# A two-layer graph network on one core: the last pair's reset gates by seven block products, the first load of x in two parts, and new scheduling constants

## The chip, the cores and the metric

The kernel runs on one core of a Trainium2 chip. The metric is device time in microseconds (us) for one execution; lower is better. A core has five instruction streams that matter here. TensorE (PE, with its weight loads as PEld) multiplies. VectorE (DVE), ScalarE (ACT) and GpSimd (POOL) work on elements. SyncE (SP) issues most of the DMAs; ScalarE's queue issues a few at the start. Each stream runs its instructions in the order in which they were written for it, and waits at the head when an input is not there yet.

## The reference, cut to what matters

The inputs are x (64 graphs, 256 nodes, 256 features) and a 0/1 adjacency of 64 matrices of 256 by 256. All arithmetic is float32.

```python
# layer 0
h = relu(bn(conv1d(xT, conv1_w)))                 # 1x1 convolution over the features
h = bn(conv1d(h, conv2_w, pad=8))                 # 17 taps over the nodes
x_conv = relu(h + xT).T
s = x @ w_se.T + b_se                             # 3 coordinates of each node
A = exp(-dist(s, s)) * adj
x_nmp = A @ relu(x @ w_msg.T + b_msg)             # message pass
x_in = concat([x_conv, x_nmp])
gi, gh = x_in @ w_ih.T + b_ih, x @ w_hh.T + b_hh  # each has parts r, z, n
r = sigmoid(gi_r + gh_r); z = sigmoid(gi_z + gh_z)
n = tanh(gi_n + r * gh_n)
x = layernorm(x + (1 - z) * n + z * x)
# layer 1
h = layernorm(x)
conv = (adj @ h) @ W_rel + b_rel + h @ W_root
out = layernorm(x + x + relu(conv))
```

## The kernel before, in words

**Tiling.** Activations lie transposed, features on the 128 partitions (two chunks, C = 2), nodes along the free axis. The 64 graphs are 8 blocks of 8; a block is 4 pairs, so there are 32 pairs. Pair 31 is the last one.

**Stages.** At the start `conv1(0)` reads the first block's x pair by pair (`fetch`, L811 to L827), transposes it on TensorE (`turned`, L829 to L848: eight transposes of 128x128 into two banks named `ps_xTc`, one ScalarE copy for each bank, one store to the buffer `xt` in memory), and runs the 1x1 convolution (`ps_c`, L866) with the weights `w1`. The weights and the batch norm's numbers (`chan`) come through ScalarE's DMA queue (L494, L495). Then `filters` turns the 17 taps into 47 filter matrices: weights `wt` are loaded, copied by VectorE (`ws`, L560), transposed (`ps_tT`, L569, copy on ScalarE L571), multiplied by a constant matrix (`ps_w`, L590) and evicted by ScalarE (L596); the result `w2m` is stored to memory. From then on, for each block, the 17-tap convolution is a transform of the activations (VectorE, L707 and others), 47 products with the filters (`ps_k`, L735) and a transform back. The filters are streamed in two-slot ring `cs` by SP's queue (`cs<-w2m`, 105 loads of 768 KB). Beside it, conv1 of the block after next runs.

**A pair.** `pair(p)` computes messages (`ps_msg`, L1105), distances (`ps_dist`, L1142), the exponential (ScalarE, L1146), the product with adj (VectorE, L1149), and the message pass (`ps_nmp`, L1156, evicted by ScalarE at L1158). Then come the gates. RG holds the reset gate and the hidden part of n; ZN holds the update gate and the input part of n. In the usual pairs the 2x2 block products of weights and activations are done as seven products instead of eight (`product`, L1198; banks `ps_a`, `ps_b`, `ps_d`): VectorE prepares differences of activation blocks (L1175 to L1183), ScalarE puts a bank into RG or ZN (`put`, L1220 and L1222), VectorE adds banks on (`onto`, L1226), and ScalarE applies the tanh by which the sigmoid is computed (`squash`, L1230). Pairs 0, 1 and 31 (PLAIN) use eight plain products (`products_of`, bank `ps_g`, L1194). For pair 31 (`apart`) these go graph by graph: RG and then ZN of graph 0, then RG and ZN of graph 1; ZN goes straight from its bank into the new state (`turn_in`, L1231 to L1241). Layer 1 follows: norm (x at L1364), projection (`ps_hy`, L1383; sums on VectorE L1385), aggregation (`ps_agg`, L1397; for the last nodes L1436) and the final norm and store (L1426, L1445, L1446). In pair 31 it goes graph by graph too.

**What sets the order.** All operations are recorded with a key, a due time in planned microseconds (`prog.at`). Pair p is due at FIRST_GATES + p * PERIOD; conv1, the convolution, filter loads and coordinates have keys relative to this through the constants at L58 to L68 (for instance COORDS, W_LAG, LOAD_AHEAD, CONV1_FROM). A list scheduler (`scheduled`) then writes a static order for each engine and each queue from these keys, its own cost model and the shares of the PSUM banks. So a changed constant can move any instruction.

Of the kernel before, what the change touches and what calls it, by code (L numbers as in the profile page):

```python
# [18 lines left out]
P = 128  # L19
B, N, D = 64, 256, 256  # L20
C = D // P
# [10 lines left out]
BG = 8  # L32
# [22 lines left out]
OB, OG = 3, 64  # L55
HQ = 2 * M * C * (M + 1)
XC_SLOTS = BG + 2
FIRST_GATES, PERIOD, GATE_TIME = 115.6, 58.9, 14.5  # L58
AHEAD_FROM, AHEAD_TO, W_DEEP = -43.5, -52.5, 2
CONV1_FROM, CONV1_TO, CONV_FROM, CONV_OUT, CONV_TO = -29.4, 98.8, -11.5, -38.6, -37.2  # L60
PAIR_LEAD, FILTER_LEAD, LOAD_AHEAD = 40.6, -2.5, 17.5
SMALL_RUNS, TURN_FROM = 1.3, 2
FILTERS_TO, STORES_AT = 51.5, 52.7
KEEP = 13.3
LATE_LAG = 28.4
W_FROM, W_LAG = 2, 41.9
COORDS = 40.5
PLAIN, SUMS_FROM = (0, 1, B // 2 - 1), 2  # L68


# [349 lines left out]
def gnn_two_layers(  # L420
# [32 lines left out]
    def bank(name, share="rest"):  # L453
        return Space(name, [P, 512], "psum", share, share if share in ("conv", "gate") else None).view
# [36 lines left out]
    taps = sb("taps", [P, NM * OB], "filters")  # L491

    prog.at(0.0)
    A.dma_start(out=chan_sb, in_=chan)  # L494
    A.dma_start(out=w1, in_=w1T.rearrange("(c p) n -> p c n", p=P))  # L495
    tb = np.zeros((2, OG, NM * OB), np.float32)
    tb[:, :TAPS * OB] = np.einsum("kf,op->kofp", tap_matrix(), np.eye(OB, dtype=np.float32)).reshape(TAPS * OB, NM * OB)
    tb = tb.reshape(P, NM * OB)
# [305 lines left out]
    def conv1(b):  # L804
        def edges(h):
            G.memset(h[:, :8, :, :, M:], 0.0)
            G.memset(h[:, 8:, :, :, :1], 0.0)
        XN = {}

        def fetch(g):  # L810
            if b >= TURN_FROM:  # L811
                XN[g] = xn_ahead[:, :4 * D]
                blocks = XN[g].rearrange("p (c k i) -> p c k i", c=C, i=SQ)
                rows_of = x[b * BG + g:b * BG + g + 2].rearrange("g (b j) d -> j (g b) d", j=SQ)
                with prog.group():
                    for a in range(P // SQ):
                        for c in range(C):
                            at = c * P + a * SQ
                            SP.dma_start(out=blocks[a * SQ:(a + 1) * SQ, c], in_=rows_of[:, :, at:at + SQ])
                return  # L820
            if b > 0:
                XN[g] = xn_ahead[:, :4 * D].rearrange("p (j d) -> p j d", d=D)
            elif g >= 4:
                XN[g] = W2[:, 1, 8 + 2 * g:12 + 2 * g]
            else:
                XN[g] = cs[:, g * 512:g * 512 + 1024].rearrange("p (j d) -> p j d", d=D)
            SP.dma_start(out=XN[g], in_=x[b * BG + g:b * BG + g + 2].rearrange("g (c p) d -> p (g c) d", p=P))  # L827

        def turned(g):  # L829
            xn = XN[g]  # L830
            if b >= TURN_FROM:
                V.transpose(xTc_ahead.rearrange("p c n -> p (c n)"), xn)
                SP.dma_start(out=xt_dram[(b * BG + g) // 2], in_=xTc_ahead)
                return xTc_ahead
            if b > 0 or g == 4:
                xTc = xTc_ahead
            elif g:
                xTc = W2[:, 1, 6 * g - 12:6 * g - 8].rearrange("p (c f) o -> p c (f o)", c=C)
            else:
                xTc = cs[:, 2048:3072].rearrange("p (c n) -> p c n", c=C)  # L840
            for c in range(C):
                ps = bank("ps_xTc")
                with prog.group():
                    for j in range(4):
                        PE.transpose(ps[:, j * P:(j + 1) * P], xn[:, j, c * P:(c + 1) * P], ident, hold=[xTc[:, c]])
                A.copy(xTc[:, c, :], ps)
            SP.dma_start(out=xt_dram[(b * BG + g) // 2], in_=xTc)
            return xTc  # L848

        if b == 0:  # L850
            for g in range(0, BG, 2):
                fetch(g)
                edges(HP[:, g // 2])
        for g in range(0, BG, 2):
            h = HP[:, g // 2]
            if b > 0:
                fetch(g)
            xTc = turned(g)
            if b > 0:
                h = xn_ahead.rearrange("p (j c g k) -> p j c g k", j=M, c=C, g=2)  # L860
                edges(h)
            for o in range(C):
                ps = bank("ps_c1")
                with prog.group():
                    for c in range(C):
                        PE.matmul(ps, w1[:, c, o * P:(o + 1) * P], xTc[:, c, :], start=(c == 0), stop=(c == C - 1),  # L866
                                  hold=[h[:, :, o]])
                pv = ps.rearrange("p (g t j) -> p j g t", g=2, j=M)
                for j, at in ((0, 0), (8, 1)):
                    A.activation(h[:, j:j + 8, o, :, at:at + M], pv[:, j:j + 8],  # L870
                                 AF.Relu, bias=bn_shift[0][:, o:o + 1], scale=bn_scale[0][:, o:o + 1])
            if b == 0:
                fold(g // 2)
            else:
                SP.dma_start(out=hd(b * BG // 2 + g // 2), in_=xn_ahead)
# [210 lines left out]
    def pair(p):  # L1086
# [75 lines left out]
        V.tensor_add(xc, xc, xT)  # L1162
        A.activation(xc, xc, AF.Relu)
        ins = (xT, nmp, xc)
        right = []
        for v, t, when in zip(ins, (tx, nmps, tc_), (due - 28, due - 10, due - 20)):
            prog.at(when, 0.3)
            b11, b12, b21, b22 = (v[:, c, g, :] for c in range(C) for g in range(2))
            if p in PLAIN:
                right.append((b11, b12, b21, b22))  # L1170
                continue
            t1, t2, t4 = (t[:, i, :] for i in ((0, 5, 6) if v is nmp else range(3)))
            t3 = t[:, 3, :] if v is xT else b12
            if v is xT:
                V.tensor_sub(t[:, 0::3], v[:, :, 1, :], v[:, 0])  # L1175
            elif v is nmp:
                V.tensor_sub(t[:, 0:3:2], t[:, 2:5:2], t[:, 1:3])
            else:
                V.tensor_sub(t1, b12, b11)
            V.tensor_sub(t2, b22, t1)  # L1180
            V.tensor_sub(t4, b21, t2)
            if v is xc:
                V.tensor_sub(t3, b22, b12)  # L1183
            right.append((b11, b21, b22, t4, t1, t2, t3))

        def products_of(ps, f, g, second, ks):
            gates = (((0, (0, 2, 1)), (2, (0,))), ((1, (0, 2, 1)), (2, (2, 1))))[second]
            with prog.group():
                for h, (gate, sources) in enumerate(gates):
                    for s in (s for s in sources if s in ks):  # L1190
                        for k in range(C):
                            left = (0, 1, 6, 3)[2 * f + k]
                            block = A21[0] if left == 6 else WB[:, left]
                            PE.matmul(ps[:, h * N:(h + 1) * N], block[:, s, gate, :], right[s][2 * k + g],  # L1194
                                      start=0 in ks and h == 0 and s == sources[0] and k == 0,
                                      stop=s == sources[-1] and k == C - 1, skip_group_check=True)

        def product(ps, i, second, start):  # L1198
            gates = (((0, (0, 2, 1)), (2, (0,))), ((1, (0, 2, 1)), (2, (2, 1))))[second]
            left, at = i, i  # L1200
            if p in PLAIN:
                f, k, g = i
                left, at = (0, 1, 6, 3)[2 * f + k], 2 * k + g
            block = A21[0] if p in PLAIN and left == 6 else WB[:, left]
            with prog.group():
                for h, (gate, sources) in enumerate(gates):
                    for j, s in enumerate(sources):
# [32 lines left out]
            stt(r, z, 3.0, r, op0=ALU.add, op1=ALU.mult)  # L1240
            stt(wT[:, i], n, 4.0, r)  # L1241

        if plain:
            prog.at(due, 2 * GATE_TIME / 44)
            for gs in ((0,), (1,)) if apart else ((0, 1),):
                for T in (RG, ZN):
                    for f in range(C):
                        for g in gs:
                            a = bank("ps_g", "gate")
                            for ks in ((0, 1), (2,)) if not apart else ((0, 1, 2),):  # L1250
                                products_of(a, f, g, T is ZN, ks)
                            if T is ZN and apart:
                                turn_in(f, g, a)
                            else:
                                put(T, f, g, a)
                        if not (T is ZN and apart):
                            squash(T, f, gs)
        else:
            for T in (RG, ZN):
                second = T is ZN  # L1260
                prog.at(due + second * GATE_TIME, GATE_TIME / 21)
                a = bank("ps_a", "gate")
                product(a, 0, second, True)
                put(T, 0, 0, a)
                b_ = bank("ps_b", "gate")
                product(b_, 1, second, True)
                onto(T, 0, 0, b_)
                product(a, 5, second, False)
                put(T, 0, 1, a)
                d = bank("ps_d", "gate")  # L1270
                product(d, 4, second, True)
                product(a, 6, second, False)
                put(T, 1, 1, a)
                onto(T, 1, 1, d)
                product(d, 2, second, False)
                onto(T, 0, 1, d)
                product(a, 3, second, False)
                put(T, 1, 0, a)
                for f in range(C):
                    squash(T, f, (0, 1))  # L1280

        prog.at(due + 2 * GATE_TIME, 0.3)
        pieces = [slice(0, 4)]
# [290 lines left out]
```

## Time and profile before

| | |
|---|---|
| median of 3 runs | 1990.72 us (1989.74 to 1990.74) |
| the profiled execution's own time | 1990.39 us |
| its span | 1988.6 us |
| granted TensorE clock, mean | 0.999 |
| TensorE busy | 1974.2 us (99%) |
| VectorE busy | 1710.0 us (86%) |
| ScalarE busy | 1006.7 us (51%) |
| GpSimd busy | 275.3 us (14%) |
| DMA | 273.14 MB, 137 GB/s |

Times within the profile are counted from the start of its span. A float32 matmul appears there as two records. In the groups and on the timeline "ps_k<-XF,cs" means that ps_k is written from XF and cs; "idle before <- releaser" is how long the engine stood idle before the instruction and what ended that. The ends of matmuls are modelled, so a TensorE that is busy in the profile can still be waiting a little; the starts are measured.

### The profile page before, as it was taken

What the parts mean: (1) busy time and instruction counts of PE and PEld (TensorE: products, weight loads), DVE (VectorE), ACT (ScalarE), POOL (GpSimd) and SP (SyncE); (2) the same over time, 40 slices, a digit from 0 to 9 for tenths busy, and PEclk for the clock granted to TensorE, in tenths of its full rate; (3) what the DMA queues carried; (4) which work ended last, traced back from release to release, by engine and by line L of the source; (5) the groups of instructions that cost most, each with busy time, mean ns of one, the idle gap of its engine ahead of it and who ended that gap; (6) DMA issues with size and microseconds to landing.
All of it is one profiled execution on the core that took longest, in us unless ns stands there. A gap on an engine that the chain in (4) does not pass through costs nothing.

```text
span 1988.6 us, 28895 instructions
## 1 busy us (share of the span) xinstructions
PE 1974.2 (99%) x10212; PEld 1604.6 (81%) x10212; DVE 1710.0 (86%) x2674; ACT 1006.7 (51%) x2342; POOL 275.3 (14%) x504
## 2 busy tenths in 40 slices
PE   9999999999999999999999999999999999999998
PEld 6887789777887788878887788877888788887875
DVE  6896998999989999899998999899988999985655
ACT  7545342754456543475345644475444653465432
POOL 1000110210110211111110111111111021111101
PEclk9999999999999999999999999999999999999999
DMA  8954555446545465445553545544554334422221
GB/s 219 309 169 127 139 170 140 126 108 186 136 141 149 110 184 143 130 132 135 184 153 109 142 140 171 146 136 112 156 149 150 99 84 158 126 77 77 76 54 43
DMA packets 461089, 273.14 MB, mean 137 GB/s; under 512 B 258192, under 2 KB 445584, under 8 KB 460944
## 3 DMA queue, kind: packets, MB, share of 16 engines
q1 hardware_dynamic: 460384, 270.94, 47.1%
q8 instruction: 81, 1.33, 0.3%
q14 instruction: 64, 0.52, 0.1%
q10 hardware_dynamic: 560, 0.34, 0.1%
HBM read 194.01 MB, written 77.20 MB: 136 GB/s over the span
## 4 chain that ended last, share of the span: by engine, by line
PE 97%; ACT 1%; DVE 1%; DMA 1%; issue 0%; SPq 0%; POOLq 0%; POOL 0%; ACTq 0%; DVEq 0%
PE ps_a L1208 22%; PE ps_k L735 17%; PE ps_d L1208 11%; PE ps_hy L1383 11%; PE ps_c L866 6%; PE ps_nmp L1156 6%; PE ps_msg L1105 6%; PE ps_b L1208 6%; PE ps_agg L1397 5%; PE ps_g L1194 5%; PE ps_dist L1142 1%; ACT w2all L596 1%; PE ps_w L590 1%; ACT tT L571 0%; DMA w<-in_w1T_dram 0%
## 5 line engine op out<-in xcount | busy, mean ns | idle before, releaser
L735 PEld LDWEIGHTS ps_k<-XF,cs 128*128 128x128 f32 x2632 | 311.8, 192 | 14.7 <-issue 8.7
L735 PE MATMUL ps_k<-XF,cs 128*128 128x128 f32 x2632 | 313.3, 275 | 0.0
L1383 PE MATMUL ps_hy<-wrr,wT 128*128 128x512 f32 x496 | 226.8, 595 | 0.0
L1208 PE MATMUL ps_a<-nmp,WB 128*128 128x256 f32 x696 | 207.0, 379 | 0.0
L1383 PEld LDWEIGHTS ps_hy<-wrr,wT 128*128 128x128 f32 x496 | 91.6, 190 | 89.8 <-issue 83.0
L1208 PE MATMUL ps_a<-tx,WB 128*128 128x256 f32 x522 | 156.0, 381 | 2.0 <-ACT ZN L1220 2.0
L1222 ACT ACTIVATE RG<-ps_a,bhh 128x512 f32<-128x512 f32 x116 | 79.2, 683 | 142.8 <-PE ps_a L1208 140.6
L1208 PEld LDWEIGHTS ps_a<-nmp,WB 128*128 128x128 f32 x696 | 132.2, 190 | 18.0
L1220 ACT COPY ZN<-ps_a 128x512 f32<-128x512 f32 x116 | 67.6, 582 | 149.4 <-PE ps_a L1208 148.8
L707 DVE TENSOR_TENSOR XF<-XF 128x512 f32<-128x512 f32 (+3 forms) x128 | 125.8, 1002 | 10.0 <-ACT XF L788 8.6
L1105 PE MATMUL ps_msg<-wms,xT 128*128 128x260 f32 x512 | 133.2, 383 | 0.0
L1156 PE MATMUL ps_nmp<-AT,msg 128*128 128x256 f32 x512 | 118.8, 379 | 0.0
L1385 DVE SCALAR_TENSOR_TENSOR HY<-ps_hy,q,hrow 128x512 f32<-128x512 f32 x124 | 92.7, 748 | 30.2 <-PE ps_hy L1383 24.9
L1397 PE MATMUL ps_agg<-HY,adja 128*128 128x256 f32 x504 | 117.2, 379 | 0.0
L1208 PEld LDWEIGHTS ps_a<-tx,WB 128*128 128x128 f32 x522 | 96.5, 190 | 24.7 <-issue 9.3
L1397 PEld LDWEIGHTS ps_agg<-HY,adja 128*128 128x128 f32 x504 | 95.1, 190 | 23.6 <-issue 10.9
L1156 PEld LDWEIGHTS ps_nmp<-AT,msg 128*128 128x128 f32 x512 | 96.8, 190 | 15.9 <-issue 2.9
L1105 PEld LDWEIGHTS ps_msg<-wms,xT 128*128 128x128 f32 x512 | 94.7, 190 | 14.9 <-issue 2.6
L866 PE MATMUL ps_c<-xTc,w 128*128 128x512 f32 x232 | 105.9, 594 | 0.0
L1208 PE MATMUL ps_a<-xc,WB 128*128 128x256 f32 x348 | 103.5, 379 | 0.0
L1208 PE MATMUL ps_a<-tc,WB 128*128 128x256 f32 x348 | 103.5, 379 | 0.0
L1208 PE MATMUL ps_d<-nmp,WB 128*128 128x256 f32 x348 | 103.5, 379 | 0.0
(226 smaller groups left out, 4254.7 us busy)
## 6 DMA issues: line engine op xcount, KB each, us to landing
cs<-w2m SPq DMA_DIRECT2D x105, 768.0 KB
adjm<-in_adjT_dram SPq DMA_DIRECT2D x64, 256.0 KB
xT<-xt SPq DMA_DIRECT2D x32, 512.0 KB
adja<-in_adjT_dram SPq DMA_DIRECT2D x64, 256.0 KB
out_dram<-HY SPq DMA_DIRECT2D x63, 256.0 KB
hd<-xn SPq DMA_DIRECT2D x28, 544.0 KB
XF<-hd SPq DMA_DIRECT2D x28, 544.0 KB
xt<-xTc SPq DMA_DIRECT2D x29, 512.0 KB
```

Source lines behind the costliest of these rows:

```text
L707: (V.tensor_add if add else V.tensor_sub)(sl(o, n), sl(a, n), sl(b, n))
L735: PE.matmul(ps[:, o * P:(o + 1) * P], w(m, c)[:, o * P:(o + 1) * P], X[:, slot, c * P:(c + 1) * P], start=first and o == 0 and c == 0, sto ...
L866: PE.matmul(ps, w1[:, c, o * P:(o + 1) * P], xTc[:, c, :], start=(c == 0), stop=(c == C - 1), hold=[h[:, :, o]])
L1105: PE.matmul(ps[:, :D + 4], xT[:, c, g, m * P:(m + 1) * P], wms[:, c, :], start=(c == 0), stop=(c == C - 1 and not idle), hold=[msg[:, g, m]])
L1156: PE.matmul(ps[:, d * N:(d + 1) * N], msg[:, g, m, d * P:(d + 1) * P], AT[:, g, m, :], start=(m == 0), stop=(m == C - 1), hold=[nmp[:, :, g]])
L1194: PE.matmul(ps[:, h * N:(h + 1) * N], block[:, s, gate, :], right[s][2 * k + g], start=0 in ks and h == 0 and s == sources[0] and k == 0, ...
L1208: PE.matmul(ps[:, h * N:(h + 1) * N], block[:, s, gate, :], right[s][at], start=start and h == 0 and j == 0, stop=j == len(sources) - 1, s ...
L1220: A.copy(o, ps)
L1222: A.activation(o, ps, AF.Identity, bias=bhh[:, 2, f:f + 1])
L1383: PE.matmul(ps, wT[:, 2 * f + g, m * P:(m + 1) * P], wrr[:, f, :], start=(f == 0), stop=(f == C - 1), hold=[HY[:, g, m]], need=[q[:, 1, j: ...
L1385: stt(HY[:, g, m, :], ps, q[:, 1, j:j + 1], hrow)
L1397: PE.matmul(ps[:, n_ * D:(n_ + 1) * D], adja[:, g, m, n_ * P:(n_ + 1) * P], HY[:, g, m, :D], start=(m == 0), stop=(m == C - 1))
```

## The change

Three things are changed.

1. `w1` is loaded ahead of `chan` on ScalarE's queue. The first pair's x (512 KB) comes in two DMAs of one graph each, and its eight transposes are grouped by graph, four and four; each group writes half of both banks, so the two ScalarE copies come after the second group.
2. In the last pair, RG of both graphs is computed together by the seven products; ZN follows with plain products, graph 0 and then graph 1, with `turn_in` as before. The differences of activation blocks that the seven products need are made by VectorE into the tiles X[28..40), four for each of the three inputs.
3. The scheduling constants get new values, among them FIRST_GATES, GATE_TIME, and the starts and ends of the stages. PERIOD stays at 58.9 and the ring's depth W_DEEP at 2.

```diff
-FIRST_GATES, PERIOD, GATE_TIME = 115.6, 58.9, 14.5
-AHEAD_FROM, AHEAD_TO, W_DEEP = -43.5, -52.5, 2
-CONV1_FROM, CONV1_TO, CONV_FROM, CONV_OUT, CONV_TO = -29.4, 98.8, -11.5, -38.6, -37.2
-PAIR_LEAD, FILTER_LEAD, LOAD_AHEAD = 40.6, -2.5, 17.5
+FIRST_GATES, PERIOD, GATE_TIME = 112.9, 58.9, 14.3
+AHEAD_FROM, AHEAD_TO, W_DEEP = -49.4, -96.2, 2
+CONV1_FROM, CONV1_TO, CONV_FROM, CONV_OUT, CONV_TO = -34.3, 126.5, -18.6, -38.7, -34.3
+PAIR_LEAD, FILTER_LEAD, LOAD_AHEAD = 39.7, 0.1, 16.5
 SMALL_RUNS, TURN_FROM = 1.3, 2
-FILTERS_TO, STORES_AT = 51.5, 52.7
-KEEP = 13.3
-LATE_LAG = 28.4
-W_FROM, W_LAG = 2, 41.9
-COORDS = 40.5
+FILTERS_TO, STORES_AT = 52.0, 48.0
+KEEP = 13.2
+LATE_LAG = 30.3
+W_FROM, W_LAG = 2, 44.1
+COORDS = 36.9
...
+    A.dma_start(out=w1, in_=w1T.rearrange("(c p) n -> p c n", p=P))
     A.dma_start(out=chan_sb, in_=chan)
-    A.dma_start(out=w1, in_=w1T.rearrange("(c p) n -> p c n", p=P))
...
-            SP.dma_start(out=XN[g], in_=x[b * BG + g:b * BG + g + 2].rearrange("g (c p) d -> p (g c) d", p=P))
+            for k in range(2) if b == 0 and g == 0 else ():
+                SP.dma_start(out=XN[g][:, 2 * k:2 * k + 2], in_=x[k].rearrange("(c p) d -> p c d", p=P))
...
+            if b == 0 and g == 0:
+                pss = [bank("ps_xTc") for _ in range(C)]
+                for k in range(2):
+                    with prog.group():
+                        for c in range(C):
+                            for j in (2 * k, 2 * k + 1):
+                                PE.transpose(pss[c][:, j * P:(j + 1) * P], xn[:, j, c * P:(c + 1) * P], ident,
+                                             hold=[xTc[:, c]])
+                for c in range(C):
+                    A.copy(xTc[:, c, :], pss[c])
...
+        for i, (v, t, when) in enumerate(((v, X[:, 28 + 4 * i:32 + 4 * i], due - 28) for i, v in enumerate(ins)) if p == B // 2 - 1 else ()):
+            prog.at(when, 0.3)
+            b11, b12, b21, b22 = (v[:, c, g, :] for c in range(C) for g in range(2))
+            blocks_of.append((b11, b12, b21, b22))
+            t1, t2, t3, t4 = (t[:, i] for i in range(4))
+            V.tensor_sub(t1, b12, b11)
+            V.tensor_sub(t2, b22, t1)
+            V.tensor_sub(t4, b21, t2)
+            V.tensor_sub(t3, b22, b12)
+            right.append((b11, b21, b22, t4, t1, t2, t3))
...
+        def seven(T):
...
+        if apart:
+            seven(RG)
+            prog.at(due + GATE_TIME, 2 * GATE_TIME / 44)
+            for g in range(2):
+                for f in range(C):
+                    a = bank("ps_g", "gate")
+                    products_of(a, f, g, True, (0, 1, 2))
+                    turn_in(f, g, a)
```

`seven(T)` holds the sequence of products, puts and additions that stood in the usual pairs' branch; that branch now calls it twice, with the same operations.

## The prediction

> **What bounds the kernel now.** I read the page's busy times and the chain that ended last first, to see which engine sets the end; then a table of windows cut where the work changes; then TensorE's waits; then the timeline of the three places that the change touches.
>
> ```profile
> PE 1974.2 (99%) x10212; PEld 1604.6 (81%) x10212; DVE 1710.0 (86%) x2674; ACT 1006.7 (51%) x2342; POOL 275.3 (14%) x504
> PE 97%; ACT 1%; DVE 1%; DMA 1%; issue 0%; SPq 0%; POOLq 0%; POOL 0%; ACTq 0%; DVEq 0%
> ```
>
> TensorE is busy for 99% of the span and is 97% of the chain. So a microsecond of matmuls is a microsecond of time, except where another engine holds TensorE. The windows tell where that is (columns: length, then busy time and count of PE, PEld, DVE, ACT, POOL, then granted clock, DMA share, GB/s):
>
> ```profile
> 0.00:7.07 7.07, 4.93 (x25) 4.46 (x25) 1.44 (x12) 2.36 (x3) 3.46 (x17) 1.00 0.74 226
> 7.07:24.68 17.61, 17.55 (x63) 9.21 (x63) 8.96 (x14) 10.80 (x22) 1.99 (x4) 1.00 0.96 261
> 24.68:65.54 40.86, 39.51 (x426) 30.84 (x425) 37.83 (x47) 39.46 (x88) 4.36 (x5) 1.00 0.87 237
> 65.54:1968.00 1902.46, 1900.43 (x9664) 1553.69 (x9665) 1648.67 (x2559) 948.85 (x2221) 261.54 (x474) 1.00 0.46 135
> 1968.00:1988.60 20.60, 11.73 (x40) 6.41 (x38) 13.14 (x42) 5.20 (x10) 3.92 (x5) 0.91 0.19 65
> ...
> PE ps_agg L1436 <- ACT x L1364: 2.0, 1, 2.0
> PE ps_a L1208 <- ACT ZN L1220: 2.0, 3, 0.7
> ...
> PE ps_c L866 <- DMA w<-in_w1T_dram: 0.9, 1, 0.9
> ```
>
> Until 7.07 nothing but warm-up and eight transposes runs. From 7.07 to 24.68 (conv1 of the first block) TensorE is full. From 24.68 to 65.54 (filters) ScalarE is busy 39.46 of 40.86 us, by its evictions: this stage is ScalarE's, although PE, whose ends are modelled, also looks busy. From 65.54 on TensorE is full: about 1900 us with three waits of 0.7. Then comes a tail of dependent steps. The stage that costs is named by this, not by the mean.
>
> **The change, part by part.** Counts of instructions come from laying the two programs' orders side by side: TensorE 4 matmuls of 128x256 fewer, VectorE 15 operations more, ScalarE 2 fewer, SP's queue one DMA more, POOL's work unchanged. The rest is order.
>
> *First x in two loads, w1 ahead of chan.*
>
> ```profile
> 0.72 0.44 ACTq L494 DMA_DIRECT2D chan<-in_chan_dram  x1
> 0.72 1.00 SPq L827 DMA_DIRECT2D cs<-in_x_dram  x2
> 1.18 0.55 ACTq L495 DMA_DIRECT2D w<-in_w1T_dram  x1
> 4.97 0.94 PEld L845 LDWEIGHTS ps_xTc<-ident,cs 128*128 128x128 f32 x8 [0.41 <-issue]
> 7.07 3.67 PE L866 MATMUL ps_c<-cs,w 128*128 128x512 f32 x8 [0.92 <-DMA w<-in_w1T_dram]
> 9.06 1.02 ACT L870 ACTIVATE XF<-ps_c,bnsh,bnsc 128x256 f32<-128x256 f32 x2 [2.24 <-PE ps_c L866]
> ```
>
> The first convolution waits for w1, not for x. w1's issue goes from 1.18 to 0.72: at most 0.46 earlier. But x then competes with w1 from the first byte: the DMA share of the first seven microseconds is already 0.74 at 226 GB/s. Before, x (512 KB) came at about 4.9, when its transposes start, and w1 at about 7.0. If w1's 256 KB now lie wholly ahead of x's end, then at the 0.35 MB/us that these loads show (w1 and a second x, 0.79 MB, between 4.9 and 7.1) x comes about 0.7 later, at 5.6; after it come four transposes (half of 0.94), a hop of some 0.2 and one copy (0.5), so about 6.85. Gain 0.2. If x is not delayed, w1 decides: gain 0.46. I take 0.3; bounds 0 (both share badly) and 0.75 (the copies' end, 6.3, decides). The split itself costs one more DMA issue on SP's queue (0.5 of it by the x2 row, hidden: the next x was used only from 10.6). chan comes later: its four small operations took 4.04 to 5.9, the consumer is the activation at 9.06, so it is covered by about 3 us; if the cover goes, the price is the excess, and conv banks stand between.
>
> The Trainium skill, page "DMA: Bandwidth & Descriptors", section "Queues, rings and completion order", says that each DMA engine takes turns between the queues that have work, a packet at a time. By that rule w1 takes half of the first x's rate, which speaks against the first part: the gain would be 0.2 and the sum −0.7, where undisturbed loads would give 0.46 and −1.0; the row of w1 landing beside a second x fits sharing, though not an even one.
>
> *Transposes of the second conv1 pair moved into the filter stage.* Eight transposes at 0.109 (x8 in 0.87 us on the timeline) leave the full part and enter a stage in which TensorE waits for ScalarE: −0.87. Their store to `xt` on SP's queue goes along, ahead of a reader past 76, hidden. Their two ScalarE copies (0.535 each) move too; one falls inside ScalarE's own stage: +0.53. In the same stage the last `ws` copies of VectorE now stand ahead of a long group (the 4.49 us of L707), behind which ScalarE had idled:
>
> ```profile
> 60.31 0.64 DVE L560 COPY ws<-wt 128x612 f32<-128x612 f32 x2
> ...
> 63.76 1.08 ACT L596 COPY w2all<-ps_w 128x423 f32<-128x423 f32 x2 [0.69 <-PE ps_w L590]
> ```
>
> −0.69. Together with the copy −0.16; bounds −0.7 (copy falls in an idle gap) and +1.0 (idle stays, and loads of `xn`, now issued ahead of the `w2m` stores, come no earlier).
>
> *Reset gates of the last pair by seven products.* Plain RG is 32 matmuls of 128x256, the seven products are 28. Each costs 0.432 (four of the records in ps_g's rows start every 0.865 us, two to a matmul): −4 × 0.432 = −1.73. VectorE gets 12 subtractions (0.42 each, rows of L1179 to L1183) and 3 additions (0.685, L1226): 7.1 us more where it is busy 20.81 of 40 us (1920 to 1960); the first products use untouched blocks, so the subtractions have 3.5 us before the third product. Hidden; if not, a late one costs its 0.4. ScalarE loses two squashes; it isn't the bound here.
>
> *What stands between distance and message pass.* In the changed order the last pair's five `ps_d` matmuls come before `ps_dist`, and `ps_nmp` follows `ps_dist` at once. Before:
>
> ```profile
> 1920.16 0.71 PE L1142 MATMUL ps_dist<-lr 4*128 4x256 f32 x8
> 1921.26 1.56 ACT L1146 ACTIVATE AT<-ps_dist,ns 128x256 f32<-128x256 f32 x4
> 1922.12 0.69 DVE L1149 TENSOR_TENSOR AT<-AT,adjm 128x512 f32<-128x512 f32 x1 [0.54 <-ACT AT L1146]
> 1923.07 3.62 PE L1156 MATMUL ps_nmp<-AT,msg 128*128 128x256 f32 x16
> ```
>
> The exponentials and the product with adj lay under 2.2 us of `ps_d` (1920.81 to 1923.07). With no work between, TensorE waits: from dist's start to nmp's start took 2.91 here, and 2.47 at the second pair (175.89 to 178.36), where the chain ran promptly; less dist's own 0.65 that is 1.8 to 2.25. ScalarE's order has a tanh (0.72) ahead of the exponentials, so up to 2.6. I take +2.1. Queued behind the waiting nmp on TensorE is all that is left, so nothing is won back; VectorE and ScalarE gain slack.
>
> *Plain update gates graph by graph, and the tail.* The matmuls are the same 40. From the third of the four gate groups on, the order on TensorE, VectorE and ScalarE is the old one, so the 2.0 wait at L1436 and the 9 us behind it stay: 0.
>
> *Constants.* The order in the steady state shifts, with no matmul added. Where I compare how much TensorE work lies between a result and its reader, only the filter ring (`cs<-w2m`, two slots) is shorter, three times in the first block: 5.95 to 6.8 us against 7.0. These loads took 4.4 to 6.8 us from issue to landing and start about 0.2 after the slot is free: 0 to 1.3 us, I take +0.2. On SP's queue the xT load of the second pair now follows the first pair's at once; the first was issued at 66.9, landed near 73 and was read at 76.3, and the new order reads it some 2.5 us sooner after its issue: of 3.3 us of slack 0.8 stays, so 0, at worst +1.0. The three waits at ps_a stay: 0.
>
> Sum: −0.3 − 0.16 − 0.87 − 1.73 + 2.1 + 0.2 = **−0.8**. The profiled execution took 1990.39 (span 1988.6 and 1.8 around it), 0.33 below the median of 1990.72; from it I get **1989.6**.
>
> **Rivals.**
> 1. *The filter ring holds TensorE in the steady state* (slower). For: reuse is as close as 7.0 us of work, and a load needs up to 0.2 + 6.8; SP's queue is in order, and some loads were issued 3 to 4.6 us late behind a waiting head. The new constants reorder that queue. Against: 273 MB at a DMA share of 0.46 leave room, and no wait of ps_k for a load is in the waits now. It decides from an issue held over 2.2 us at such a place: some 2.5 us per block, in five of eight blocks 12.5: about 2002.
> 2. *No nmp wait*, because the chain runs ahead by other work: 1989.6 − 2.1 = 1987.5. Against: dist stands directly before nmp in TensorE's order.
> 3. *Start and filter gains don't arrive* (loads share, ScalarE still bounds, transposes' copies in its stage): start 0, filter stage +0.5, rest as above: 1990.39 + 0.5 − 0.87 − 1.73 + 2.1 + 0.2 = 1990.6.
> 4. *No nmp wait and the three ps_a waits gone too:* 1985.5. Against: their places in the order are the same.
>
> That the matmuls are not saved can be excluded by the count.
>
> **How the numbers follow.** Forecast 0.62; rival 1 0.09, rival 2 0.08, rival 3 0.17, rival 4 0.04. About 0.2% (4.0 us: 1986.7 to 1994.7) is what a measurement can tell from no change. The forecast with all gains at their best (−0.75 − 0.7 − 0.87 − 1.73 + 1.8) is 1988.1, with all at their worst (0 + 1.0 − 0.87 − 1.73 + 2.6 + 1.3 + 1.0) 1993.7, and hardly all together. The range goes from 1986.9 (rival 2 with a better start) to 1993.0 and leaves out rivals 1 and 4. Faster: rival 4 and a little of 2, 0.06. Slower: rival 1 and a little for several blocks' short waits, 0.12. The rest, 0.82, is the same.
>
> **What would show it.** Of after: one wait of ps_nmp for VectorE's AT near 1920, 1.8 to 2.6 us; first ps_c at about 6.8; first ps_k some 0.5 earlier; PE busy about 1972; the waits of ps_agg (2.0) and ps_a (three of 0.7) unchanged; no wait of ps_k for `cs`. Wrong if ps_k waits for DMA, if the waits at ps_a grow in number, or if the tail after the last matmul isn't 9 us.

## The result, and the profile after

The changed kernel takes 1993.58 us (median of 18 runs, 1991.30 to 1995.73); the kernel before, on the same chips, 1989.93 us (18 runs, 1989.35 to 1990.82). The ratio is 1.0017, with a 95% interval of 1.0011 to 1.0023: 3.65 us slower. That is less than 0.2%, but it has the wrong sign, and it lies 0.6 us above the range (1986.9 to 1993.0). The runs also lie further apart: 4.4 us instead of 1.5. By their spans they form two groups: six at 1989.5 to 1990.5 us, all with a mean granted clock of 0.999, and twelve at 1991.4 to 1994.0 us, all at 0.997 or 0.998.

The profiled execution took 1994.69 us, with a span of 1991.8 us, against 1988.6 before; another 1.0 us of its time lies outside the span (2.8 us instead of 1.8) and is not explained here. First the page's busy times and chain, then the waits of TensorE, of the changed kernel:

```profile
PE 1974.8 (99%) x10204; PEld 1604.9 (81%) x10204; DVE 1718.3 (86%) x2689; ACT 1012.8 (51%) x2340; POOL 274.6 (14%) x504
PE 97%; ACT 2%; DVE 1%; DMA 1%; issue 0%; POOLq 0%; POOL 0%; SPq 0%; DVEq 0%; ACTq 0%
...
PE ps_nmp L1169 <- DVE AT L1162: 2.2, 2, 1.6
PE ps_agg L1462 <- ACT x L1390: 2.0, 1, 2.0
PE ps_a L1228 <- ACT ZN L1240: 2.0, 3, 0.7
PE ps_k L735 <- DMA cs<-w2m: 1.2, 1, 1.2
```

TensorE issues the eight records (four matmuls) fewer that were counted, and yet it is busy for 0.6 us longer. Busy time that grows while work shrinks says that some matmuls ran slower. Two waits are new: ps_nmp (two places) and ps_k on a filter load. The old ones, ps_agg and the three at ps_a, are as they were.

The timeline of TensorE at the last pair, and windows across the same place (columns: length, busy time and count of PE, PEld, DVE, ACT, POOL, then the granted clock, the DMA share, GB/s):

```profile
1923.86 0.71 PE L1155 MATMUL ps_dist<-lr 4*128 4x256 f32 x8
1926.21 5.41 PE L1169 MATMUL ps_nmp<-AT,msg 128*128 128x256 f32 x16 [1.64 <-DVE AT L1162]
1931.45 0.59 PE L1228 MATMUL ps_a<-xT,WB 128*128 128x256 f32 x2
...
1923.00:1926.00 3.00, 1.57 (x13) 0.78 (x11) 2.04 (x4) 2.90 (x7) 0.00 (x0) 1.00 0.51 175
1926.00:1927.00 1.00, 0.79 (x2) 0.70 (x3) 0.85 (x2) 1.00 (x3) 0.00 (x0) 0.66 0.00 0
1927.00:1928.00 1.00, 1.00 (x4) 0.73 (x4) 0.59 (x1) 0.98 (x2) 0.00 (x0) 0.50 0.00 0
1928.00:1929.00 1.00, 1.00 (x4) 0.82 (x3) 0.93 (x3) 0.00 (x0) 0.00 (x0) 0.50 0.00 0
1929.00:1930.00 1.00, 1.00 (x5) 0.80 (x4) 1.00 (x2) 0.07 (x1) 0.00 (x0) 0.63 0.00 0
1930.00:1931.00 1.00, 1.00 (x6) 0.89 (x5) 0.15 (x1) 0.51 (x1) 0.00 (x0) 1.00 0.00 0
```

This is the main reading. The sixteen ps_nmp records begin at 1926.21, after 1.64 of waiting, and the next product begins at 1931.45: they take 5.24 us, where they took 3.45 before (1923.07 to 1926.52). The granted clock falls to 0.50 just as they begin and is back at 1.00 some 3.4 us later. The wait is paid once as idle time and once more as slow matmuls.

Six places that both timelines show tell where the 3.2 us of the two spans came from (times of the same instruction, before and after):

| place | before | after | after minus before |
|---|---|---|---|
| first ps_c matmul | 7.07 | 7.06 | 0.0 |
| ps_a that waits for ZN, near 1591 | 1591.32 | 1592.38 | +1.1 |
| ps_a that waits for ZN, pair 30 | 1917.81 | 1919.34 | +1.5 |
| ps_nmp of the last pair starts | 1923.07 | 1926.21 | +3.1 |
| first gate matmul behind it | 1926.52 | 1931.45 | +4.9 |
| last ps_agg | 1979.61 | 1982.80 | +3.2 |

So up to pair 30 the new order costs 1.5; the wait ahead of ps_nmp adds 1.6, the half clock 1.8; and the gates give 1.7 back. The busy time fits this: 1974.2 - 1.7 for the matmuls saved + 1.8 for the half clock here + 0.5 for a shorter one under the last ps_agg (2.66 us instead of 2.17, without moving the end of the span) is 1974.8.

### The profile page after: what moved, and what is told of

The parts are those of the page before. It is cut to its first block, busy times and chain, and to the rows that moved or that the text cites. A ratio compares the mean times of both kernels' runs of the same rounds, so it can differ in the third digit from the quotient of the medians.

```text
span 1991.8 us, 28946 instructions
## 1 busy us (share of the span) xinstructions
PE 1974.8 (99%) x10204; PEld 1604.9 (81%) x10204; DVE 1718.3 (86%) x2689; ACT 1012.8 (51%) x2340; POOL 274.6 (14%) x504
## 4 chain that ended last, share of the span: by engine, by line
PE 97%; ACT 2%; DVE 1%; DMA 1%; issue 0%; POOLq 0%; POOL 0%; SPq 0%; DVEq 0%; ACTq 0%
PE ps_a L1228 23%; PE ps_k L735 17%; PE ps_d L1228 11%; PE ps_hy L1409 11%; PE ps_b L1228 6%; PE ps_nmp L1169 6%; PE ps_msg L1118 6%; PE ps_c L879 5%; PE ps_agg L1423 5%; PE ps_g L1217 4%; PE ps_dist L1155 1%; ACT w2all L596 1%; ACT tT L571 0%; PE ps_w L590 0%; DMA cs<-w2m 0%
```

## The experiments

The scheduler makes large changes out of small ones, so most kernels here are edited behind it: `move(ops, before)` takes operations out of the written order and puts them ahead of another one, and nothing else moves.

Theory 1: the cost is the idle time ahead of ps_nmp and the half clock behind it, and, smaller, late filter loads. Theory 2: the cost is in the steady state. Theory 3: ps_nmp is slow because other engines work beside it.

| run | what | median, us (runs) | lowest to highest |
|---|---|---|---|
| after | the changed kernel | 1993.58 (18) | 1991.30 to 1995.73 |
| e1 | distances early | 1991.07 (11) | 1990.22 to 1991.84 |
| e2 | wait filled with idle matmuls | 1992.38 (11) | 1991.31 to 1993.20 |
| e3 | two filter loads first | 1992.44 (11) | 1990.56 to 1993.56 |
| e4 | e1 and e3 | 1990.39 (11) | 1989.23 to 1991.39 |
| e5 | before, with the distances late | 1993.39 (11) | 1991.44 to 1994.33 |
| e6 | before, tail filled | 1989.71 (11) | 1989.59 to 1990.14 |
| e7 | e4, two more products moved, tail filled | 1988.94 (11) | 1988.07 to 1990.15 |
| e8 | new code, old constants | 1997.18 (5) | 1997.10 to 1997.50 |
| e9 | e7 with the first x in one load | 1988.40 (11) | 1987.49 to 1990.15 |
| e10 | old code, new constants | 2000.54 (5) | 1998.55 to 2002.35 |
| e11 | as e2, a quarter of the filling | 1992.46 (1) | |
| e12 | as e2, half of the filling | 1991.37 (1) | |

The kernel before measured 1989.93 beside e1 to e4, 1990.13 beside e5 to e8 and 1990.66 beside e9 to e12.

**e1: the distances early.**

```diff
     order = scheduled(prog.ops)
...
+    move([dist], d_op)            # ps_dist of pair 31 ahead of the five ps_d matmuls
...
+    move(exps, first_act)         # its exponentials ahead of three L1452 and an L1250
+    move([muls[0]], onto_d)       # product with adj, graph 0, ahead of L1246
```

> The changed kernel with the order altered only at the last pair's distances: ps_dist stands ahead of the five ps_d matmuls again, the four exponentials ahead of three layer norm activations and a tanh on ScalarE, and the product of graph 0 with adj ahead of one addition on VectorE. Theory 1 (the idle time of TensorE before ps_nmp, and the half clock that follows it, are the main cost): ps_nmp no longer waits (2.0 us gone), its 16 records take 3.45 us again and not 5.24 (1.8 gone), time 1993.6 - 3.8 = 1989.8; 1990.5 if the clock does not fall in every run. Theory 2 (the cost lies in the steady state, in loads that the new constants put late): the last pair is worth 1 us at most and the time stays at 1992.6 to 1993.6. Theory 3 (ps_nmp is slow because ScalarE and VectorE work beside it): the wait goes, the slow matmuls stay, 1991.6.

Measured: 1991.07, 2.5 less than the changed kernel (expected: 3.8). TensorE's timeline:

```profile
1921.01 0.71 PE L1155 MATMUL ps_dist<-lr 4*128 4x256 f32 x8
...
1923.92 1.89 PE L1169 MATMUL ps_nmp<-AT,msg 128*128 128x256 f32 x8
1926.19 1.99 PE L1169 MATMUL ps_nmp<-AT,msg 128*128 128x256 f32 x8 [0.38 <-DVE AT L1162]
```

The first half no longer waits, and the granted clock stays at 1.00 up to the last matmul. The second half waits 0.38: graph 1's product with adj was left behind an addition on VectorE, and that is part of the missing 1.3. The rest is probably that the clock falls at ps_nmp in some two thirds of the changed kernel's runs only (twelve of 18 by the groups above). Theory 2 is out as the main cause: it allowed 1 us here.

**e2: the wait filled.** The same wait, but TensorE multiplies something useless during it.

```diff
+    nmp_op = nth(1169, -2)
+    name, method, args, named, at_line = nmp_op.calls[0]
+    for k in range(8):
+        nmp_op.calls.insert(0, (name, method, (args[0][:, :P], args[1], args[1]), {"start": True, "stop": True}, at_line))
```

> The changed kernel with eight idle matmuls of 128x128 (some 1.8 us, their result overwritten) put into the wait between ps_dist and ps_nmp of the last pair, nothing else moved. Theory 1: ps_nmp starts as late as before, 2.35 us after ps_dist, but the granted clock stays at 1.00 and its 16 records take 3.45 us: 1.8 us less, 1991.8 (up to 1992.5 if the clock falls in some runs only). Theory 3 (work of other engines slows ps_nmp): still 5.2 us, 1993.6. Theory 2: 1993.6 as well.

Measured: 1992.38. The timeline of e2, and the window of its real ps_nmp records:

```profile
1924.44 0.71 PE L1155 MATMUL ps_dist<-lr 4*128 4x256 f32 x8
1925.09 2.05 PE L1169 MATMUL ps_nmp<-msg 128*128 128x128 f32 x16
1926.97 3.62 PE L1169 MATMUL ps_nmp<-AT,msg 128*128 128x256 f32 x16
1930.43 0.59 PE L1228 MATMUL ps_a<-xT,WB 128*128 128x256 f32 x2
...
1926.97:1930.43 3.46, 3.46 (x18) 3.05 (x17) 2.87 (x5) 2.19 (x4) 0.00 (x0) 1.00 0.00 0
```

The idle matmuls take the 1.9 us that were idle, and the sixteen real records take 3.46 (1926.97 to 1930.43) at a granted clock of 1.00. The same work on ScalarE and VectorE lies beside them (2.2 and 2.9 us busy; in the changed kernel 2.4 and 3.4 in the longer stretch), so theory 3 falls: it is the idle time that slows them. The gain of 1.2 instead of 1.8 fits a clock that falls in some two thirds of the runs. In this kernel's own profile the half clock came in the tail instead (the last eight ps_agg records: 3.60 against 2.17 in before).

**e3: filter loads first.** In the second and the third block the third load goes ahead of four small stores on SP's queue.

```diff
+    loads = [o for o in order if line_of(o) == 728]
+    for k in (18, 34):
+        at = order.index(loads[k])
+        small = [o for o in order[at - 20:at] if line_of(o) == 1143][0]
+        order.remove(small)
+        order.insert(at, small)
```

> The changed kernel with two filter loads (the third load of the second and of the third block) put ahead of the four small stores of coordinates on SP's queue, nothing else moved. Theory 1 with its smaller part: the load of the third block is issued 2.6 us sooner, the 1.2 us for which ps_k waited for it are gone, 1992.3. Theory 2 would have more such waits in other runs than the profiled one and gain more, 1991. If the queue is not what holds the load, no change: 1993.6.

Measured: 1992.44, 1.1 less. SP's queue and the ps_k that reads the load, first in the changed kernel, then in e3:

```profile
685.68 3.28 SPq L1350 DMA_DIRECT2D x<-wd  x4
689.01 2.52 SPq L1143 DMA_DIRECT2D sd<-turned  x4
691.62 0.53 SPq L728 DMA_DIRECT2D cs<-w2m  x1
...
698.04 2.13 PE L735 MATMUL ps_k<-XF,cs 128*128 128x128 f32 x17 [1.21 <-DMA cs<-w2m]
```

```profile
685.64 3.94 SPq L1350 DMA_DIRECT2D x<-wd  x4
689.62 0.60 SPq L728 DMA_DIRECT2D cs<-w2m  x1
690.26 2.48 SPq L1143 DMA_DIRECT2D sd<-turned  x4
...
696.63 2.62 PE L735 MATMUL ps_k<-XF,cs 128*128 128x128 f32 x22
```

No gap shows on SP's queue here; it is busy issuing. Each small DMA takes it 0.6 to 1.0 us, and eight of them stand in a row ahead of the load. In the new order the four stores of coordinates stand right in front of it; COORDS sets their due time, but no run changed COORDS alone. Issued 2.0 us sooner, the load is there in time. The wait is not always 1.2: other profiles with the late load show 0.7 (e2), 0.6 (e12) or none (e11) at this place.

**e4: both.** The edits of e1 and e3 together.

> Both changes of order of the two runs before in one kernel. Theory 1: the gains add, 1993.6 - 3.8 - 1.2 = 1988.6, 1.3 us below the kernel before. Theory 2: 1991 to 1992.4. Theory 3: 1990.4.

Measured: 1990.39, 3.2 less than the changed kernel; e1 and e3 alone give 2.5 and 1.1, so they add but for 0.5. With two repairs of order the kernel is back at the time of before, not below it. Left in its profile are two waits at ps_nmp (1.0 in all, one of them in pair 30, which is new too) and half the clock in the tail.

**e5: the wait put into the kernel before.**

```diff
     order = scheduled(prog.ops)
...
+    move([d_op], dist)            # the five ps_d matmuls ahead of ps_dist of pair 31
```

> The kernel before with one thing moved: the five ps_d matmuls of pair 30 stand ahead of ps_dist of the last pair, so that ps_nmp follows ps_dist at once. Theory 1: from ps_dist to ps_nmp some 2.5 us, of which 1.8 to 2.0 idle, and then the half clock for some 3 us: 1989.9 + 1.9 + up to 1.8, so 1992.5 to 1993.6. If the idle time alone counts: 1991.8. If such a wait is won back later (theory 2, the end is set elsewhere): 1989.9 to 1990.5.

Measured: 1993.39, 3.3 above the kernel before, by one move of five matmuls. The timeline and windows of e5 repeat the picture:

```profile
1922.04 0.71 PE L1142 MATMUL ps_dist<-lr 4*128 4x256 f32 x8
1924.39 5.31 PE L1156 MATMUL ps_nmp<-AT,msg 128*128 128x256 f32 x16 [1.64 <-DVE AT L1149]
...
1922.00:1924.00 2.00, 0.75 (x9) 0.31 (x8) 0.36 (x1) 1.23 (x4) 0.00 (x0) 1.00 0.00 0
1924.00:1926.00 2.00, 1.61 (x4) 1.34 (x5) 2.00 (x4) 1.80 (x4) 0.00 (x0) 0.56 0.11 37
1926.00:1928.00 2.00, 2.00 (x7) 1.60 (x6) 0.13 (x1) 0.00 (x0) 0.00 (x0) 0.59 0.67 225
```

Its eleven runs fall into two groups: four at 1991.4 to 1991.9, six at 1993.4 to 1994.3, and one at 1992.6. The lower group lies where the idle time alone would put it (1.6 above the kernel before), the upper one where the half clock comes on top. So the same wait seems to cost 1.6 or 3.7, from run to run. The half clock was seen in the profiled run (1993.39); for the others it is inferred from the times, since the mean granted clock of a run, which also counts the time after the last matmul, is 0.998 or 0.999 in both groups.

**e6: the tail of before filled.** Eight idle matmuls in the 2.0 us wait ahead of the last ps_agg, as in e2.

> The kernel before with eight idle matmuls of 128x128 (1.8 us, result overwritten) in the 2.0 us wait ahead of the last ps_agg. Theory 1 (an idle stretch of 2 us puts the clock down for some 3 us, at a moment that changes from run to run): the last eight ps_agg records always take 1.73, the median falls by 0 to 0.7, to between 1989.2 and 1989.9, and the runs lie closer together. Rival (the clock falls after the last matmul anyway): 1989.9 with the same spread.

Measured: 1989.71, against 1990.13 beside it, and the eleven runs lie within 0.55 us instead of 1.5. The interval of the ratio (0.9988 to 1.0006) holds no change, but the spread shrinks to about a third. That fits a clock that falls in the last microseconds of some runs: from the start of the last ps_agg to the end of the span it took 9.63 in e2 and 9.76 in e4, where the clock fell there, and 8.98 to 9.05 in before, e1, e3 and e5, where it did not. No profile of the kernel before shows such a run.

**e7: the order mended.** The edits of e4, the filling of e6, and:

```diff
+    mul30 = nth(1162, -4)
+    at = order.index(mul30)
+    move([mul30], [o for o in order[at - 14:at] if line_of(o) == 1246][-1])
...
+    move([muls[1]], onto_d)
```

> The changed kernel with the distances early and the filter loads first as before, and three more changes of order: VectorE's product with adj of pair 30's graph 0 ahead of one addition, that of the last pair's graph 1 too, and the eight idle matmuls in the wait ahead of the last ps_agg. Theory 1: 1990.4 less 0.8 (ps_nmp's wait in pair 30) less 0.5 (ps_nmp's second wait in the last pair) less 0.5 to 1.0 (half clock in the tail): 1988.1 to 1988.6, below the kernel before by 1.3 to 1.8. If the waits of VectorE come back one step later: 1989.5 to 1990.

Measured: 1988.94, 1.2 below the kernel before beside it (ratio 0.9994, interval 0.9985 to 1.0003, so not clear of it). No wait of ps_nmp is left in its waits. The products with adj were behind an addition and another operation on VectorE for no reason of data.

**e8 and e10: code and constants crossed.** The new code with the old constants, and the reverse; the scheduler writes a new order for each.

> The changed code (two loads of x, w1 first, seven products for the reset gates) with the constants of before. In its order ps_dist stands ahead of five ps_d matmuls. Theory 1 (the products save 1.73, the loads nothing, the cost is the new order): 1989.9 - 1.7 = 1988.2. If the seven products themselves cost something in the last pair (waits for VectorE's differences): 1989.9 to 1991. If the loads were what costs: 1991 or more.

> The code of before with the new constants. In its order ps_dist of the last pair stands ahead of five ps_d matmuls, so the 2.0 us wait and the half clock behind it are not there. Theory (the constants alone bring late filter loads and pair 30's wait, and the transposes into the filter stage): 1989.9 + 1.2 + 0.8 - 0.4 = 1991.5. If the new constants are good in themselves and only the last pair's code spoils it: 1989.5 or less. If they are as bad with the old gates as the old ones are with the new gates (e8): 1994 or more.

Measured: 1997.18 and 2000.54. Both are far off what was expected, the first the wrong way; of the second only the last alternative (1994 or more) came true. The waits of TensorE in e8 and then in e10:

```profile
PE ps_agg L1423 <- DVE HY L1403: 5.3, 1, 5.3
PE ps_a L1228 <- ACT ZN L1240: 2.0, 3, 0.7
PE ps_agg L1462 <- DVE HY L1403: 1.9, 1, 1.9
```

```profile
PE ps_a L1208 <- ACT ZN L1220: 3.2, 3, 1.8
PE ps_wT L1338 <- DVE wT L1241: 3.0, 1, 3.0
PE ps_c L866 <- ACT xTc L846: 2.1, 1, 2.1
PE ps_agg L1436 <- DVE HY L1377: 1.9, 1, 1.9
```

In e8 the cost is one wait of 5.3 in the tail, ending at 1978.65, and half the clock from 1975.47 to 1982.30. A likely reason, not tested, is that graph 0's update gates come later in the new code, and the old due times no longer put enough work between them and the last aggregations. In e10 the longer waits are at 62 to 64 (conv1 matmuls that wait for a copy), at one ps_a and in the tail, and the clock falls to half behind two of them (from 63.88 and from 1978.76). Two of the changed kernel's costs are in e10 and not in e8: a wait of ps_k for a filter load (0.8) and the one of ps_nmp in pair 30 (0.6); so they come with the new constants. The largest, ps_nmp's 1.64 in the last pair, is in neither: only code and constants together put ps_dist behind the five ps_d matmuls. So the times of code and constants cannot be added up as two effects: together they cost 3.65, alone 7 and 10. What the new constants do right in the tail is shown by the changed kernel itself, whose tail is the old one to 0.1 us; which of the eighteen changed constants does it was not tried.

**e9: the first x in one load again,** in e7, with `chan` ahead of w1.

```diff
+    move([chan_op], w1_op)
...
+    x0.calls = [(name, method, args, {"out": x_all, "in_": whole}, at_line)]
+    order.remove(x1_)
```

> The mended order of e7 with the first x in one load again and chan ahead of w1 on ScalarE's queue (the eight transposes stay in their two groups). Theory (the two loads gain nothing because w1 and x share the DMA engines from the start): the first ps_c matmul starts at 6.3 to 7.1 in both, time 1988.9, within 0.4. If the two loads gain what the prediction took: 1989.2 to 1989.4. If w1 first delays x by more than it gains: 1988.5.

Measured: 1988.40, against 1990.66 for the kernel before beside it: ratio 0.9989, interval 0.9980 to 0.9998. This is the one kernel here that is faster than the kernel before by more than its interval. Against e7 it is 0.5 lower, within the spread; that the two loads gain anything is not to be seen. In its profile the first ps_c came at 7.43, later than the expected 6.3 to 7.1 and than e7's 7.12, so that execution shows no gain at the start either.

**e11 and e12: how long may TensorE idle?** As e2, with two and four idle matmuls.

> The changed kernel with two idle matmuls of 128x128 (0.45 us) at the start of the wait between ps_dist and ps_nmp, so that 1.5 us of idle time are left. How long must TensorE idle for the clock to fall? The three waits of 0.84 at ps_a never did it, the one of 2.0 did it each time. If a length between counts: at 1.5 us ps_nmp still takes 5.2 us. If it is the moment that counts and not the length: 3.45 in some runs, 5.2 in others.

> As e11 with four idle matmuls (0.9 us), so that 1.1 us of idle time are left. If the threshold lies between 1.1 and 2.0 us: ps_nmp takes 3.45 us at the full clock here. If it lies between 0.84 and 1.1: 5.2 us.

```profile
1925.89 3.72 PE L1169 MATMUL ps_nmp<-AT,msg 128*128 128x256 f32 x16 [0.99 <-DVE AT L1162]
```

With a wait of 0.99 (e11) and of 0.55 (e12) ps_nmp runs at the full clock: 3.72 by the profile's ends, close to the 3.62 of before, against 5.41 in the changed kernel. The idle matmuls left less of a wait than the 1.5 expected of e11. One execution each, so this says only that a wait of 1.0 can pass without the clock falling. The waits at ps_a, called 0.84 in the expectation, are 0.68 on the timeline, and the one of 2.0 in the tail did not put the clock down each time.

The traces of these runs say more on length against moment. Within each trace the steps of the granted clock lie on a grid of 3.41 us: in the changed kernel 1926.33, 1929.74 and 1984.35, which is once and sixteen times 3.413 apart. Half the clock lasts one such stretch, or two (6.83, behind e8's wait of 5.3). Against the kernel the grid lies elsewhere in each execution. The 2.0 us wait in the tail passed at the full clock in before, e1, e3, e5 and e12, where a step of the grid cut it into pieces of at most 1.78; it put the clock down in the changed kernel, e2, e4 and e11, where 1.86 to 2.05 of it lay in one stretch. Even the 1.82 us wait at ps_a in e10, cut into 1.06 and 0.76, passed (timeline, then the two stretches):

```profile
1597.22 0.70 PE L1208 MATMUL ps_a<-tx,WB 128*128 128x256 f32 x2 [1.82 <-ACT ZN L1220]
...
1593.05:1596.46 3.41, 2.35 (x11) 1.72 (x10) 3.34 (x7) 2.88 (x13) 0.41 (x1) 1.00 0.04 11
1596.46:1599.87 3.41, 2.65 (x14) 2.11 (x18) 3.38 (x6) 0.90 (x4) 2.93 (x3) 1.00 0.00 0
```

So by these traces the idle time inside one stretch decides, and the border lies near half of it (e10's last wait put the clock down with 1.74, by modelled ends). At ps_nmp 1.48 to 1.64 in one stretch was enough. There the ps_dist matmuls (0.7 us, four rows of 128 in use) stand in the same stretch and may count as idle, which no run separates. An estimate on that assumption: with 2.35 us from ps_dist to ps_nmp and a border of 1.75, a grid that lies at random puts the clock down in two thirds of the runs, as in twelve of 18 of the changed kernel.

## Why the prediction was wrong, point by point

- **The wait between distance and message pass, "+2.1": this is the step that failed.** Place and cause were right, and the idle time was even shorter than forecast (2.35 us from ps_dist to ps_nmp, expected 2.47 to 2.91; 1.64 of it idle, expected 1.8 to 2.6). What was missing is a second price: after it the granted clock was 0.50 for 3.4 us, and ps_nmp took 5.24 instead of 3.45. Wait and slow matmuls cost 1.6 + 1.8 = 3.4. The last window of before, with a granted clock of 0.91, held a hint that the prediction read over: there the clock fell at 1984.91, 3.1 us after the last matmul, so an idle TensorE can lose it; that a wait of 2 us can be enough it did not show, as the matmuls behind the wait of 2.0 ran at the full clock.
- **The filter ring, "+0.2", and rival 1.** The mechanism of rival 1 is what happened: SP's queue held a load for at least 2.0 us (e3 issued it that much sooner). But it was at one place, not in five blocks, the queue was busy and not waiting at its head, and it cost 1.2 in the profile (e3's median: 1.1 less). The prediction compared how much TensorE work lies between slot and reader, and found it shorter in the first block only; it did not look at what stands ahead of the load on SP's queue, where the new order has four stores of 0.6 us each.
- **Pair 30, not in the sum.** ps_nmp waits 0.6 there too; the order on VectorE puts a product with adj behind an addition. It is part of the +1.5 at 1919.34. With the ring's wait taken out (e3), the wait at ps_a of 1591 comes at 1590.90 instead of 1591.32 in before, so up to there the change gains 0.4. Counted from the first ps_c, whose own start changes from run to run, it is the same: 1583.9 in e3, e4, e7 and e9, 1584.3 in before, e5 and e6.
- **Start, "−0.3": 0.0.** Conv1 began at 7.06 against 7.07. In the changed kernel the second half of x came at 5.95 and w1 no longer decided:

```profile
5.95 0.66 PE L850 MATMUL ps_xTc<-ident,cs 128*128 128x128 f32 x4 [0.67 <-DMA cs<-in_x_dram]
7.06 3.70 PE L879 MATMUL ps_c<-cs,w 128*128 128x512 f32 x8 [0.46 <-ACT cs L853]
```

  That is the later of the two ends from which 0.3 was chosen (5.6), and later still. The Trainium skill, page "DMA: Bandwidth & Descriptors", section "Queues, rings and completion order", with its queues that share an engine in turns, was the better guide; this trace fits it, x's second half being 1.0 us later than the whole x was before. (With a gain of 0.46 the sum is −0.9, not the −1.0 of the prediction.) The reading that w1 decides held for one execution of the kernel before only: with the same start, e5, e6 and e10 had their first ps_c at 6.76, 6.24 and 6.91, behind the copies and not behind w1, for instance e6:

```profile
6.24 1.98 PE L866 MATMUL ps_c<-cs,w 128*128 128x512 f32 x4 [0.24 <-ACT cs L846]
```

  The changed start gave 6.82 to 7.17 in nine profiles. By these profiles the start had nothing to gain.
- **Transposes and filter stage, "−0.87 − 0.16".** The first ps_k came at 65.55 against 65.47, with the eight transposes done, so they were free as forecast. But ps_k then waited 0.35 for ScalarE's last filter evictions, which one of the transposes' own copies (0.6) stands ahead of. Of 1.03, some 0.4 arrived by 1591.
- **The seven products, "−1.73": right.** From the first gate matmul (1926.52 and 1931.45) to the last ps_agg (1979.61 and 1982.80) the distance shrank by 1.74. VectorE's subtractions stayed hidden: no wait for them in the list.
- **Tail and the three waits at ps_a, "0": right** in the profile (from the last ps_agg to the end 9.05 against 8.99). e2 and e4 show that the tail can cost 0.6 to 0.8 more when the clock falls there.
- **Together.** Wait +1.3, ring +1.0, pair 30 +0.6, start +0.3 and transposes +0.6, each against its term, turn the forecast −0.8 into +3.0; the two spans lie 3.2 apart.
- **The range.** All costs at their worst were summed to 1993.7, and the range cut at 1993.0. With the half clock as a cost of 0 to 1.8 it would have held the time. That the uncut 1993.7 holds it would have been luck: it was made of other costs.

The Trainium skill, page "TensorE: Matmul & The Clock Gate", section "Part 1: The HAM clock gate", says that the array's clock is halved after an idle window of about 3.4 us, that the window runs freely and is not started by the kernel, and gives as a rule to leave no idle gaps above that. Half the clock for 3.41 us, the grid of 3.41 us and the change from run to run are in the traces here, so they agree with the window. As a threshold for an idle gap the 3.4 us do not hold here: 1.64 us of waiting, 2.35 from the four-row ps_dist matmuls to ps_nmp, were enough in most runs.

## What to carry to other kernels

On a kernel whose TensorE is full, price a new wait twice: its length, and, once it comes to 1.6 us or more as here, the matmuls behind it at half the clock for 3.4 us, in some runs and not in others; a run-to-run spread that grows with a change can be a sign of it, and a few useless matmuls in the wait show it in one run. When a constant moves small DMAs, look at what stands behind them on the same queue: eight issues of 0.6 to 1.0 us delay a load as surely as a blocked head. And where a scheduler writes the order, keep its order and move single operations to find a cause; e8 and e10 show that the time of half a change tells little, though its waits show which half a cost comes with.

## What the runs showed of the hardware that was not expected

A wait of TensorE of 1.64 us brought the granted clock to 0.50 for 3.4 us in three profiles of three (the changed kernel, e3, e5), and by the groups of e5's times, an inference, in some six of eleven runs; waits of 0.7, 0.99 and, once, 1.82 did not. The 2.0 us wait in the tail did it before the last matmuls in some executions (3.60 for eight ps_agg records in e2) and not in others (2.17 in e5), by where it lay on the clock's grid of 3.41 us. Filling that one wait narrowed the runs of the kernel before, otherwise unchanged, from 1.5 us to 0.55.
